# Layer 0's output turned by VectorE and DRAM, and layers 0 and 1 in another order of steps

## The chip, the cores and the metric

The kernel runs on one core of a Trainium2 chip. The metric is the device time of one execution, in microseconds (us). The profile is one execution taken by the hardware profiler. Engines are named as in the profile: PE is TensorE's matmuls, PEld its weight loads, DVE is VectorE, ACT is ScalarE, POOL is GpSimd, SP is SyncE, which here only issues DMAs.

## What is computed

Four layers of a graph network over 128 graphs of 64 nodes with 256 features each, all in float32. Every layer ends in a residual and a layer norm. The change concerns the first two:

```python
# layer 0: attention over a dense 64 x 64 adjacency
Wh = h @ W
e = leaky_relu(Wh @ a1 + (Wh @ a2)^T)          # masked where adj == 0
x = layernorm(x + softmax(e) @ Wh)
# layer 1: attention over a list of 512 edges (src, dst), 4 heads
Xq = H @ W_lin.T ; Xv = H @ W_val.T
e = (leaky_relu(Xq[src] + Xq[dst]) * a).sum(d) + log(adj[src, dst] + 1e-8)
attn = softmax of e over the edges of a src
x = layernorm(x + segment_sum(attn * Xv[dst], src) @ W_out.T)
# layer 2: two matmuls with batch norm over all rows; layer 3: two graph products and four LSTMs
```

Layer 2's batch norm needs all rows, so layers 0 and 1 are finished for all graphs before the rest of layer 2 runs.

## The kernel before

**Blocks.** The 8192 rows (128 graphs of 64 nodes) are cut into NQ = 16 blocks of QT = 512 rows, eight graphs in each. `A` is one large SBUF tile with a slot of 1024 floats per partition for each block. It holds each block's values as they pass through the layers; until a slot is needed, it also serves as scratch memory for the setup (`su`).

**Two layouts.** A matmul contracts over partitions. So the projections `h @ W` need their rows turned: features on partitions, rows along the free dimension. In *token-major* layout the rows are on partitions.

- `transposed` (L199 to L206) turns a block with TensorE: eight transposes of 128x128 (L204) into two PSUM banks, and two evictions by ScalarE (L205) into the tile `tT`.
- Layer 0's input for blocks 1 to 15 is turned otherwise. `load_x` (L126 to L135) loads the block twice: once token-major into `xin` (L128), and once into the block's slot of `A` in 32x32 squares (L135), by eight DMAs of 64 KB each, whose rows of 32 floats are put so that squares lie at their turned places. VectorE's transpose (L220 in `l0_a`) then turns each square in itself, which completes the turn.
- Layer 1's input, the output of layer 0, is turned by TensorE for all blocks (`l1_t`, L285).

**Steps of layer 0** for a block: `l0_a` turns the input; `l0_b` projects it (L230); `l0_c` makes the scores, starting with four TensorE transposes (L241), and their exponentials; `l0_d` turns those (L260); `l0_e` multiplies by them (L270), adds the residual (L273), takes the layer norm's statistics on VectorE, and lets GpSimd normalise into the slot of `A` (L83 and L97). `load_x(q + 2)` follows there.

**Steps of layer 1**: `l1_t` turns; `l1_qv` projects to queries (L295) and values (L298) in two halves; eight `l1_graph`, one per graph, gather the queries along the edges (L332) and apply a relu on ScalarE (L334); `reduce_heads` (called by `sums`, L323) sums it up. Over two blocks (BPS = 2) together, `l1_softmax`, `l1_sums` and `l1_weights` make the attention with scans on VectorE, turn it (L366), let GpSimd scatter it into a table in DRAM (four indirect DMAs, L378), and load the table back (`ld`, L384, two DMAs of 512 KB). `v_a` has GpSimd copy a block's attention from `ld` to `am` (L391), multiplies the values by it (L399) and empties the two banks on ScalarE (`yT`, L403). `v_b` multiplies by `W_out` (L413), adds the residual (L415), normalises on GpSimd and stores the block (L418). `v_c` is the first graph product of layer 2 (L433).

**Order.** For each block the loop at L659 goes through eight slots. Each slot runs one `l1_graph`, then the steps listed for it in `between`; a step belongs to the block named with it, so layer 0 runs two blocks ahead of layer 1's graphs, and `v_a` to `v_c` run three or four behind (LAG = 3). `step` chains TensorE: the instructions that a step puts on TensorE are issued after those of the step before (`tc.issue_after`). So TensorE follows the written order, while the framework's scheduler places the instructions on the other engines, each engine working in order.

**Buffers.** The PSUM banks named `m` are three (`bank`, `bufs=3`) and serve nearly every step. `z` has two banks for `l1_graph` and `v_c`. The tile `tT` has one buffer (`bufs=1`) in `work` for layer 0 and layer 1 together.

Of the kernel before, what the change touches and what calls it, by code (L numbers as in the profile page):

```python
# [8 lines left out]
F32 = mybir.dt.float32  # L9
# [8 lines left out]
P = 128  # L18
NB = 128
N = 64  # L20
D = 256
KD = D // P
HEADS = 4
# [3 lines left out]
NQ = 16  # L27
PQ = 4
QT = 512
# [12 lines left out]
def kernel(ctx: ExitStack, tc: tile.TileContext, i, out):  # L42
    nc = tc.nc
# [4 lines left out]
    dram = ctx.enter_context(tc.tile_pool(name="dram", bufs=1, space=DRAM))  # L48
# [3 lines left out]
    A = main.tile([P, NQ, 2 * QT], F32, name="A")  # L52
# [59 lines left out]
    with ExitStack() as two:  # L112
        wa = two.enter_context(tc.tile_pool(name="wa", bufs=1))
        values, ph = ExitStack(), ExitStack()
        vp = values.enter_context(tc.tile_pool(name="vp", bufs=1, side="right"))
        psm = values.enter_context(tc.tile_pool(name="psm", bufs=1, space=PSUM, side="right"))
        xp = ph.enter_context(tc.tile_pool(name="xp", bufs=2))
        work = ph.enter_context(tc.tile_pool(name="work", bufs=2))
        ps = ph.enter_context(tc.tile_pool(name="ps", bufs=1, space=PSUM))

        def bank(shape, name="m", bufs=3):
            return (psm if name == "m" else ps).tile([P] + shape, F32, name=name, bufs=bufs)

        xin = {}

        def load_x(q):  # L126
            xin[q] = xp.tile([P, PQ, D], F32, name="xin")
            nc.sync.dma_start(xin[q], x_view[q])  # L128
            if q:

                rows = i["x"][q * QT:(q + 1) * QT, :].rearrange("(j t) (k i f) -> i k t j f", t=32, k=KD, f=32)
                for n in range(4):
                    for k in range(KD):
                        to = A[n * 32:(n + 1) * 32, q, k * QT:(k + 1) * QT]
                        nc.sync.dma_start(to.rearrange("t (j f) -> t j f", f=32), rows[n, k])  # L135

        class su:

# [27 lines left out]
        for s in range(2):  # L166
            nc.sync.dma_start(bd[s * N:(s + 1) * N, s * N:(s + 1) * N], i["adj"])
        load_x(1)

        wq = wa.tile([P, KD, D + HEADS], F32, name="wq")  # L170
        wv = wa.tile([P, KD, D], F32, name="wv")
# [26 lines left out]
        def transposed(src, q=1):  # L198

            t = own(q, [P, KD, QT], "tT")  # L200
            for k in range(KD):
                p_ = bank([PQ, P])
                for c in range(PQ):
                    nc.tensor.transpose(p_[:, c, :], src[:, c, k * P:(k + 1) * P], ident)  # L204
                nc.scalar.activation(t[:, k, :], p_.rearrange("p c t -> p (c t)"), AF.Copy)  # L205
            return t  # L206

        def token_major(q):

            return A[:, q, :].rearrange("p (c d) -> p c d", c=PQ)  # L210


        L0 = {}

        def l0_a(q):
            L0[q] = {"x": xin.pop(q)}
            if q:

                L0[q]["xT"] = work.tile([P, KD, QT], F32, name="tT", bufs=1)
                nc.vector.transpose(L0[q]["xT"].rearrange("p k t -> p (k t)"), A[:, q, :])  # L220
            else:
                L0[q]["xT"] = transposed(L0[q]["x"], q)

        def l0_b(q):
            xT = L0[q]["xT"]
            wh = L0[q]["wh"] = own(q, [P, PQ, D + 2], "wh")
            for c in range(PQ):
                p_ = bank([D + 2])
                for k in range(KD):
                    nc.tensor.matmul(p_, xT[:, k, c * P:(c + 1) * P], w0[:, k, :],  # L230
                                     start=k == 0, stop=k == KD - 1)
                nc.scalar.activation(wh[:, c, :], p_, AF.Copy)

            sb = L0[q]["sb"] = own(q, [P, PQ, P], "sb")
            nc.scalar.activation(sb, wh[:, :, D + 1:].to_broadcast([P, PQ, P]), AF.Copy)

        def l0_c(q):
            wh, sb = L0[q]["wh"], L0[q]["sb"]
# [25 lines left out]
        def l0_e(q):  # L264
            x, wh, eT, ri = (L0[q][n] for n in ("x", "wh", "eT", "ri"))
            for c2 in range(2):
                p_ = bank([2, D])
                for c in range(2):
                    g = 2 * c2 + c
                    nc.tensor.matmul(p_[:, c, :], eT[:, g, :], wh[:, g, :D], start=True, stop=True)  # L270
                for c in range(2):
                    g = 2 * c2 + c
                    nc.vector.scalar_tensor_tensor(x[:, g, :], p_[:, c, :], ri[:, g:g + 1], x[:, g, :],  # L273
                                                   op0=OP.mult, op1=OP.add)
            layernorm(token_major(q), x, PQ, nc.gpsimd)
            L0.pop(q)
            if q + 2 < NQ:
                load_x(q + 2)


        L1 = {}

        def l1_t(q):
            L1[q] = {"xT": transposed(token_major(q)), "qs": [],
                     "v": vp.tile([P, PQ, D], F32, name="v", bufs=5)}  # L285

        def l1_qv(q, c2):
            xT, v = L1[q]["xT"], L1[q]["v"]

            sp = spads[q // BPS % 2].rearrange("p (s e x b d h) -> p s e x b d h", e=2, s=2, x=2, b=BPS, d=2)  # L290
            pv = bank([2, D])
            for c in (2 * c2, 2 * c2 + 1):
                pq = bank([D + HEADS])
                for k in range(KD):
                    nc.tensor.matmul(pq, xT[:, k, c * P:(c + 1) * P], wq[:, k, :],  # L295
                                     start=k == 0, stop=k == KD - 1)
                for k in range(KD):
                    nc.tensor.matmul(pv[:, c % 2, :], xT[:, k, c * P:(c + 1) * P], wv[:, k, :],  # L298
                                     start=k == 0, stop=k == KD - 1)

                qs = work.tile([P, 2, D], F32R, name="qs", bufs=6)
                L1[q]["qs"].append(qs)
                for s in range(2):
                    r, ro = slice(s * N, (s + 1) * N), slice((1 - s) * N, (2 - s) * N)
                    nc.scalar.activation(qs[r, s, :], pq[r, :D], AF.Copy)  # L305
                    nc.vector.tensor_sub(qs[ro, s, :], pq[r, :D], qs[r, s, :].bitcast(F32))  # L306
                    nc.scalar.activation(sp[r, s, c % 2, 0, q % BPS, c // 2, :], pq[r, D:], AF.Copy, scale=SLOPE)
            nc.scalar.activation(v[:, 2 * c2:2 * c2 + 2, :], pv, AF.Copy)
# [75 lines left out]
                nc.sync.dma_start(ld[S][s * N:(s + 1) * N], half)  # L384


        def v_a(q):
            S, b = divmod(q, BPS)
            v = L1[q]["v"]
            am = vp.tile([P, PQ * HEADS, N], F32, name="am")  # L390
            nc.gpsimd.tensor_copy(am.rearrange("p (e r) n -> p e r n", e=2),  # L391
                                  ld[S].rearrange("p n (e b r) -> p b e r n", e=2, b=BPS)[:, b])
            pY = [bank([KD, PQ, N]) for _ in range(2)]
            for c in range(PQ):
                for h in range(HEADS):
                    for s in range(2):
                        r = slice(s * N, (s + 1) * N)
                        r0 = (h % 2) * 64
                        nc.tensor.matmul(pY[s][r0:r0 + 64, h // 2, c, :], v[r, c, h * 64:(h + 1) * 64],  # L399
                                         am[r, (c % 2) * 2 * HEADS + c // 2 * HEADS + h, :], start=True, stop=True)  # L400
            yT = L1[q]["yT"] = vp.tile([P, KD, PQ, 2, N], F32, name="yT")
            for s in range(2):
                nc.scalar.activation(yT[:, :, :, s, :], pY[s], AF.Copy)  # L403
# [234 lines left out]
        LAG = BPS + 1  # L638
# [20 lines left out]
        for q in range(NQ):  # L659
            S = q // BPS - 1 if q % BPS == 0 else -1  # L660
            between = [
                [(l0_e, q + 1), (l0_a, q + 2)],
                [(sums, q if q else -1), (l1_softmax, S)],
                [(l1_sums, S), (l0_b, q + 2)],
                [(v_b, q - LAG - 1)],
                [(l1_weights, S), (l1_t, q + 1), (l0_c, q + 2)],
                [(sums, q), (l1_qv, q + 1, 0)],
                [(v_c, q - LAG - 1), (v_a, q - LAG)],
                [(l0_d, q + 2), (l1_qv, q + 1, 1)],
            ]  # L670
            for b in range(GQ):
                step(l1_graph, q, b)
                for do, n, *more in between[b]:
                    step(do, n, *more)
                if setup:
                    setup.pop(0)()
        sums(q)
        S = NQ // BPS - 1
# [56 lines left out]
        q = 0  # L735
        for do, n in [(v_b, NQ - LAG - 1), (v_c, NQ - LAG - 1)] + [
                (do, n) for n in range(NQ - LAG, NQ) for do in (v_a, v_b, v_c)]:
            do(n, *[False] * (do == v_c))
            up_block(q)
            q += 1  # L740
# [85 lines left out]
    work = ctx.enter_context(tc.tile_pool(name="work3", bufs=2, reuse_waits="tile"))  # L826
# [311 lines left out]
```

## Time and profile before

| | us |
|---|---|
| median of 3 runs | 2138.15 (2138.13 to 2138.42) |
| profiled execution: span | 2136.4 |
| layers 0 and 1, up to the last graph step | about 515 |
| one pair of blocks in the steady part (four in a row) | 61.25, 61.26, 61.25, 61.26 |
| TensorE busy in such a pair | 58.3 |
| VectorE, ScalarE, GpSimd busy in such a pair | 37.5, 40.9, 23.4 |

The granted clock is 1.00 in all four of these pairs. A pair is the unit to think in: the edge attention and its table come once for two blocks. The rest of the span, from about 515 us on, is layers 2 and 3, which the change doesn't touch, apart from one separate call of the attention's copy for the last three blocks.

### The profile page before, as it was taken

What the parts mean: (1) busy time and instruction counts of PE and PEld (TensorE: products, weight loads), DVE (VectorE), ACT (ScalarE), POOL (GpSimd) and SP (SyncE); (2) the same over time, 40 slices, a digit from 0 to 9 for tenths busy, and PEclk for the clock granted to TensorE, in tenths of its full rate; (3) what the DMA queues carried; (4) which work ended last, traced back from release to release, by engine and by line L of the source; (5) the groups of instructions that cost most, each with busy time, mean ns of one, the idle gap of its engine ahead of it and who ended that gap; (6) DMA issues with size and microseconds to landing.
All of it is one profiled execution on the core that took longest, in us unless ns stands there. A gap on an engine that the chain in (4) does not pass through costs nothing.

```text
span 2136.4 us, 29441 instructions
## 1 busy us (share of the span) xinstructions
PE 2060.7 (96%) x11343; PEld 1330.1 (62%) x11343; DVE 885.9 (41%) x2069; ACT 932.1 (44%) x1795; POOL 430.1 (20%) x569
## 2 busy tenths in 40 slices
PE   5999999998999989999999999999999999999998
PEld 4666767665544444585576576577467468468467
DVE  7456566654444343333234334324324324323213
ACT  2776666664339014334234334334334334333333
POOL 1134334332210010121112112113103103102012
PEclk8999999998999989999999999999999999999999
DMA  5244532322240021012112102103103102101001
GB/s 144 63 69 73 85 61 53 52 43 43 43 118 29 0 89 60 21 54 66 40 46 74 40 29 90 40 11 99 50 6 104 50 1 89 50 1 60 20 1 60
DMA packets 232636, 113.41 MB, mean 53 GB/s; under 512 B 150192, under 2 KB 215728, under 8 KB 232240
## 3 DMA queue, kind: packets, MB, share of 16 engines
q1 hardware_dynamic: 230640, 109.57, 20.2%
q8 instruction: 89, 1.46, 0.3%
q0 software_dynamic: 1024, 1.05, 0.2%
q10 hardware_dynamic: 832, 0.92, 0.1%
q14 instruction: 51, 0.42, 0.1%
HBM read 67.45 MB, written 44.04 MB: 52 GB/s over the span
## 4 chain that ended last, share of the span: by engine, by line
PE 86%; DVE 6%; ACT 4%; issue 2%; POOL 1%; DMA 1%; SPq 0%; POOLq 0%; DVEq 0%; ACTq 0%
PE l L994 36%; PE l L1000 20%; PE pz L784 5%; PE pz L719 5%; PE e L323 3%; PE g L933 2%; PE g L945 2%; PE m L295 2%; PE m L230 2%; PE z L332 2%; PE m L298 2%; PE g L878 1%; PE m L413 1%; PE m L270 1%; ACT u L334 1%
## 5 line engine op out<-in xcount | busy, mean ns | idle before, releaser
L994 PE MATMUL l<-H,wih 128*128 128x256 f32 (+2 forms) x2496 | 787.5, 470 | 1.8 <-ACT H L957 1.2
L994 PEld LDWEIGHTS l<-H,wih 128*128 128x128 f32 x2496 | 471.4, 190 | 286.2 <-issue 185.6
L1000 PE MATMUL l<-hid,whh 128*128 128x256 f32 (+2 forms) x1536 | 435.9, 437 | 0.0
L1000 PEld LDWEIGHTS l<-hid,whh 128*128 128x128 f32 x1536 | 291.8, 190 | 128.4 <-issue 61.2
L1006 ACT ACTIVATE gate_i<-l,bias 128x256 f32<-128x256 f32 (+2 forms) x176 | 100.3, 570 | 441.9 <-PE l L1000 374.2
L1010 POOL TENSOR_TENSOR cell<-gate_f,cell 128x256 f32<-128x256 f32 (+2 forms) x96 | 85.0, 885 | 726.0 <-ACT gate_f L1006 726.0
L1009 DVE TENSOR_TENSOR gate_i<-gate_i,gate_g 128x256 f32<-128x256 f32 (+2 forms) x96 | 49.6, 517 | 415.1 <-ACT gate_g L1006 415.0
L83 POOL TENSOR_TENSOR ln_rs<-ln_rs,mhalf 128x2 f32<-128x2 f32 (+2 forms) x97 | 82.0, 846 | 571.6 <-DVE ln_rs L95 570.7
L334 ACT ACTIVATE u<-z 128x1024 f32<-128x1024 f32 x128 | 130.3, 1025 | 63.3 <-PE z L332 62.3
L1006 ACT ACTIVATE gate_g<-l,bias 128x256 f32<-128x256 f32 (+2 forms) x176 | 100.3, 570 | 107.9 <-PE l L994 59.5
L1014 ACT ACTIVATE gate_g<-cell 128x256 f32<-128x256 f32 (+2 forms) x176 | 90.0, 511 | 86.9 <-DVE cell L1013 45.0
L1013 DVE TENSOR_TENSOR cell<-gate_i,gate_g 128x512 f32<-128x512 f32 (+2 forms) x80 | 48.2, 602 | 186.5 <-ACT gate_g L1006 186.4
L1006 ACT ACTIVATE gate_o<-l,bias 128x256 f32<-128x256 f32 (+2 forms) x176 | 99.3, 564 | 59.9 <-PE l L1000 54.0
L719 PE MATMUL pz<-A,w 128*128 128x512 f32 x256 | 113.1, 595 | 0.0
L332 PE MATMUL z<-gath_r,qs 128*128 128x512 f32 x256 | 100.4, 480 | 0.7 <-ACT u L334 0.4
L306 DVE TENSOR_TENSOR qs<-m,qs 64x256 fp32r<-64x256 f32 x128 | 54.0, 422 | 107.0 <-ACT qs L305 104.8
L719 PEld LDWEIGHTS pz<-A,w 128*128 128x128 f32 x256 | 47.9, 190 | 55.3 <-issue 53.3
L295 PE MATMUL m<-wq,tT 128*128 128x260 f32 x256 | 71.8, 403 | 7.8 <-ACT yT L403 5.4
L1006 ACT ACTIVATE gate_f<-l,bias 128x256 f32<-128x256 f32 (+2 forms) x96 | 51.1, 532 | 59.6 <-PE l L1000 59.1
L1023 DVE TENSOR_TENSOR hid<-gate_o,gate_g 128x256 f32<-128x256 f32 (+2 forms) x96 | 47.4, 493 | 61.2 <-ACT gate_o L1006 35.1
L721 DVE BATCH_NORM_STATS2 st<-pz 128x6 f32<-128x512 f32 x64 | 44.4, 697 | 59.5 <-PE pz L719 59.4
L1023 DVE TENSOR_TENSOR H<-gate_o,gate_g 128x512 f32<-128x512 f32 (+1 forms) x64 | 41.3, 645 | 66.6 <-PE l L994 46.1
(242 smaller groups left out, 2525.2 us busy)
## 6 DMA issues: line engine op xcount, KB each, us to landing
way<-st SPq DMA_DIRECT2D x59, 256.0 KB
st<-way SPq DMA_DIRECT2D x236, 64.0 KB
xin<-in_x SPq DMA_DIRECT2D x16, 512.0 KB
ld<-table SPq DMA_DIRECT2D x16, 512.0 KB
x_dram<-y SPq DMA_DIRECT2D x16, 512.0 KB
x2r<-x_dram SPq DMA_DIRECT2D x32, 256.0 KB
x_dram<-A SPq DMA_DIRECT2D x64, 128.0 KB
x3r<-x_dram SPq DMA_DIRECT2D x64, 128.0 KB
```

Source lines behind the costliest of these rows:

```text
L83: nc.gpsimd.tensor_tensor(dst, dst, mhalf[:, :n], OP.pow)
L295: nc.tensor.matmul(pq, xT[:, k, c * P:(c + 1) * P], wq[:, k, :], start=k == 0, stop=k == KD - 1)
L332: nc.tensor.matmul(z[:, k, :], L1[q]["qs"][c][:, s, k * P:(k + 1) * P], gath_r, start=True, stop=True)
L334: nc.scalar.activation(u, z, AF.Relu)
L719: nc.tensor.matmul(p_, w1[:, k, m * P:(m + 1) * P], A[:, q, k * QT:(k + 1) * QT], start=k == 0, stop=k == KD - 1)
L784: nc.tensor.matmul(p_, w2[:, k, m * P:(m + 1) * P], hidden(q, k), start=k == 0, stop=k == M1 - 1)
L994: nc.tensor.matmul(gates[n], wih[p][:, k, mw * P:(mw + 1) * P], Hw[:, k, :, s, :], start=k == 0, stop=not s and k == KD - 1)
L1000: nc.tensor.matmul(gates[n], whh[p][:, k, m * P:(m + 1) * P], hid[:, k], start=False, stop=k == KD - 1)
L1006: nc.scalar.activation(act[n], gates[n], AF.Tanh if n == "g" else AF.Sigmoid, bias=bias[:, p - 1, m:m + 1])
L1010: nc.gpsimd.tensor_tensor(cell[:, j], act["f"], cell[:, j], OP.mult)
L1014: nc.scalar.activation(act["g"], cell[:, j], AF.Tanh)
L1023: nc.vector.tensor_mul(Hw[:, jj, :, s, :] if over else new[:, jj], o, t)
```

## The change

Layer 1's input is turned in the manner of layer 0's, for blocks 2 to 15 (`TURN = 2`). When `l0_e` has normalised a block, it is written to DRAM (`x1_dram`, 512 KB), and read back as 32x32 squares by eight DMAs (`load_squares`) into the next block's slot of `A`, or, for the last two blocks, into a tile named `xin`. `l1_t` then turns the squares on VectorE. The eight transposes on TensorE and the two evictions on ScalarE are gone for these blocks. It is meant to take work from TensorE, and the new order to leave time for the round trip.

Layer 0's input of block 1 is now turned by TensorE like that of block 0. The squares of x for later blocks are loaded by `load_xT`, one block at a time, once the projection of the block before has been traced (in `l0_b`), since VectorE now puts the turned tile into the next block's slot instead of into `tT`.

In the order of steps `l0_e` and the next `l0_a` go from the first slot to the last slot of the block before; the second half of the queries from the last slot to the first of the next block; `l0_b`, `v_b`, `l0_c`, `l1_t`, `l1_weights`, `v_c` and `v_a` change places as the diff shows. GpSimd's copy of the attention becomes a step of its own, `v_am`, in the fourth slot; its product `v_a` is in the eighth.

```diff
@@ load_x
-            if q:
-                rows = i["x"][q * QT:(q + 1) * QT, :].rearrange("(j t) (k i f) -> i k t j f", t=32, k=KD, f=32)
-                for n in range(4):
-                    for k in range(KD):
-                        to = A[n * 32:(n + 1) * 32, q, k * QT:(k + 1) * QT]
-                        nc.sync.dma_start(to.rearrange("t (j f) -> t j f", f=32), rows[n, k])
+        TURN = 2
+        def load_squares(to, rows):
+            rows = rows.rearrange("(j t) (k i f) -> i k t j f", t=32, k=KD, f=32)
+            for n in range(4):
+                for k in range(KD):
+                    part = to[n * 32:(n + 1) * 32, k * QT:(k + 1) * QT]
+                    nc.sync.dma_start(part.rearrange("t (j f) -> t j f", f=32), rows[n, k])
+        def load_xT(q):
+            load_squares(A[:, q, :], i["x"][q * QT:(q + 1) * QT, :])
@@ setup: after load_x(1)
+        load_xT(2)
@@ l0_a
-            if q:
-                L0[q]["xT"] = work.tile([P, KD, QT], F32, name="tT", bufs=1)
-                nc.vector.transpose(L0[q]["xT"].rearrange("p k t -> p (k t)"), A[:, q, :])
-            else:
+            if q < TURN:
                 L0[q]["xT"] = transposed(L0[q]["x"], q)
+                return
+            t = A[:, q + 1, :] if q + 1 < NQ else work.tile([P, KD * QT], F32, name="tT", bufs=1)
+            nc.vector.transpose(t, A[:, q, :])
+            L0[q]["xT"] = t.rearrange("p (k t) -> p k t", k=KD)
@@ l0_b, at its end
+            if TURN <= q + 1 < NQ:
+                load_xT(q + 1)
@@ l0_e, after layernorm(token_major(q), x, PQ, nc.gpsimd)
+            if q >= TURN:
+                x1 = dram.tile([QT, D], F32, name="x1_dram", bufs=2)
+                nc.sync.dma_start(x1.rearrange("(c p) d -> p c d", p=P), token_major(q))
+                sq[q] = A[:, q + 1, :] if q + 2 < NQ else xp.tile([P, PQ, D], F32, name="xin").rearrange(
+                    "p c d -> p (c d)")
+                load_squares(sq[q], x1)
@@ l1_t
-            L1[q] = {"xT": transposed(token_major(q)), "qs": [],
-                     "v": vp.tile([P, PQ, D], F32, name="v", bufs=5)}
+            L1[q] = {"qs": [], "v": vp.tile([P, PQ, D], F32, name="v", bufs=5)}
+            if q < TURN:
+                xT = transposed(token_major(q))
...
+                return
+            xT = work.tile([P, KD, QT], F32, name="tT", bufs=1)
+            with tc.issue_after([t for t in nc.cur_bb.bb.instructions if t.engine == mybir.EngineType.DVE][-1]):
+                nc.vector.transpose(xT.rearrange("p k t -> p (k t)"), sq.pop(q))
...
@@ v_a is cut in two
-        def v_a(q):
+        def v_am(q):
             S, b = divmod(q, BPS)
-            v = L1[q]["v"]
-            am = vp.tile([P, PQ * HEADS, N], F32, name="am")
+            am = L1[q]["am"] = vp.tile([P, PQ * HEADS, N], F32, name="am")
             nc.gpsimd.tensor_copy(am.rearrange("p (e r) n -> p e r n", e=2),
                                   ld[S].rearrange("p n (e b r) -> p b e r n", e=2, b=BPS)[:, b])
+        def v_a(q):
+            v, am = L1[q]["v"], L1[q]["am"]
@@ the order of steps, one line for each of the eight slots
-                [(l0_e, q + 1), (l0_a, q + 2)],
-                [(sums, q if q else -1), (l1_softmax, S)],
-                [(l1_sums, S), (l0_b, q + 2)],
-                [(v_b, q - LAG - 1)],
-                [(l1_weights, S), (l1_t, q + 1), (l0_c, q + 2)],
+                [(l0_e, -1 if q else 1), (l0_a, -1 if q else 2), (l1_qv, q if q else -1, 1)],
+                [(sums, q if q else -1), (l1_softmax, S), (l0_b, q + 2)],
+                [(l1_sums, S), (v_b, q - LAG - 1)],
+                [(l0_c, q + 2), (l1_t, -1 if q else 1), (v_am, q - LAG)],
+                [(l1_t, q + 1 if q else -1), (l1_weights, S)],
                 [(sums, q), (l1_qv, q + 1, 0)],
-                [(v_c, q - LAG - 1), (v_a, q - LAG)],
-                [(l0_d, q + 2), (l1_qv, q + 1, 1)],
+                [(l0_d, q + 2), (v_c, q - LAG - 1)],
+                [(v_a, q - LAG), (l0_a, q + 3 if q + 4 < NQ else -1), (l0_e, q + 2),
+                 (l0_a, q + 3 if q + 4 == NQ else -1)],
```

More of the change, by code (lines that the diff above doesn't have):

```diff
@@ L128, in load_x @@
             nc.sync.dma_start(xin[q], x_view[q])
-            if q:
-                rows = i["x"][q * QT:(q + 1) * QT, :].rearrange("(j t) (k i f) -> i k t j f", t=32, k=KD, f=32)
-                for n in range(4):
-                    for k in range(KD):
-                        to = A[n * 32:(n + 1) * 32, q, k * QT:(k + 1) * QT]
-                        nc.sync.dma_start(to.rearrange("t (j f) -> t j f", f=32), rows[n, k])
+        TURN = 2
[7 more added lines that the diff above has]
+            load_squares(A[:, q, :], i["x"][q * QT:(q + 1) * QT, :])
+        sq = {}
         class su:
@@ L283, in l1_t @@
         def l1_t(q):
-            L1[q] = {"xT": transposed(token_major(q)), "qs": [],
-                     "v": vp.tile([P, PQ, D], F32, name="v", bufs=5)}
+            L1[q] = {"qs": [], "v": vp.tile([P, PQ, D], F32, name="v", bufs=5)}
+            if q < TURN:
+                xT = transposed(token_major(q))
+                L1[q]["xT"] = [[xT[:, k, c * P:(c + 1) * P] for c in range(PQ)] for k in range(KD)]
+                return
+            xT = work.tile([P, KD, QT], F32, name="tT", bufs=1)
+            with tc.issue_after([t for t in nc.cur_bb.bb.instructions if t.engine == mybir.EngineType.DVE][-1]):
+                nc.vector.transpose(xT.rearrange("p k t -> p (k t)"), sq.pop(q))
+            L1[q]["xT"] = [[xT[:, k, c * P:(c + 1) * P] for c in range(PQ)] for k in range(KD)]
         def l1_qv(q, c2):
@@ L294, in l1_qv @@
                 for k in range(KD):
-                    nc.tensor.matmul(pq, xT[:, k, c * P:(c + 1) * P], wq[:, k, :],
+                    nc.tensor.matmul(pq, xT[k][c], wq[:, k, :],
                                      start=k == 0, stop=k == KD - 1)
                 for k in range(KD):
-                    nc.tensor.matmul(pv[:, c % 2, :], xT[:, k, c * P:(c + 1) * P], wv[:, k, :],
+                    nc.tensor.matmul(pv[:, c % 2, :], xT[k][c], wv[:, k, :],
                                      start=k == 0, stop=k == KD - 1)
@@ L737 @@
                 (do, n) for n in range(NQ - LAG, NQ) for do in (v_a, v_b, v_c)]:
+            if do == v_a:
+                v_am(n)
             do(n, *[False] * (do == v_c))
```

## The prediction

> **What bounds the kernel now.** I read the page first for the engine that never rests, then the table by stage for one repeating stretch, then TensorE's timeline in it for the holes.
>
> ```profile
> PE 2060.7 (96%) x11343; PEld 1330.1 (62%) x11343; DVE 885.9 (41%) x2069; ACT 932.1 (44%) x1795; POOL 430.1 (20%) x569
> 333.25:394.50 61.25, 58.41 (x539) 42.94 (x539) 37.10 (x96) 40.90 (x91) 23.14 (x27) 1.00 0.29 55
> ```
>
> The second line is one pair of blocks, an even and an odd one, in the steady part of layers 0 and 1 (columns: stretch, length, busy time of PE, PEld, DVE, ACT, POOL, granted clock, DMA share, GB/s). TensorE works 58.4 of 61.25 us, ScalarE 40.9, VectorE 37.1. So TensorE sets the period; the time can only change by its work or by its holes. TensorE's timeline gives both:
>
> ```profile
> 358.81 0.60 PE L366 MATMUL m<-ident,e 128*128 128x128 f32 x4
> 359.25 0.60 PE L366 MATMUL m<-ident,dn 128*128 128x128 f32 x4
> 360.52 0.79 PE L204 MATMUL m<-ident,A 128*128 128x128 f32 x4 [0.67 <-issue]
> 362.00 0.65 PE L204 MATMUL m<-ident,A 128*128 128x128 f32 x4 [0.69 <-ACT tT L205]
> 362.99 0.66 PE L241 MATMUL m<-ident,sb 128*128 128x128 f32 x4 [0.33 <-DVE ln_mv L93]
> 373.92 1.15 PE L295 MATMUL m<-wq,tT 128*128 128x260 f32 x4 [0.56 <-ACT yT L403]
> 378.13 1.89 PE L270 MATMUL m<-wh,eT 128*128 128x256 f32 x8
> ...
> 390.70 1.03 PE L204 MATMUL m<-ident,A 128*128 128x128 f32 x8
> 391.58 0.60 PE L241 MATMUL m<-ident,sb 128*128 128x128 f32 x4
> ```
>
> In the odd block the eight transposes of L204 hold TensorE from 390.70 to 391.58, 0.88 us. In the even one they stand behind the attention's own transposes (L366), which hold two of the three PSUM banks named m, and three holes of 0.67, 0.69 and 0.33 us open round them. One more hole of 0.52 to 0.56 us per block stands ahead of the second half of the queries (L295), which waits until the two banks of the value product have been emptied (yT L403). Together 2.8 us of the pair.
>
> [...] L204 needs ScalarE's L205 (0.60 us) to leave PSUM, while L220 (1.25 us for 128x1024) has its input put in place by DMA. [...] No run here shows yet how a write fares behind the large table load, and my odd block rests on it.
>
> **The change, part by part.**
>
> *Removed.* For blocks 2 to 15 eight transposes each: 2 x 0.88 = 1.76 us of TensorE per pair, and four evictions of 0.60 on ScalarE, which isn't the bound (0). With them go the three holes by the attention's transposes, since l0_c's transposes move a step ahead and nothing else wants a bank there until the next block's queries some 2.6 us later (z 0.73, sums 1.85): 1.69 per pair.
>
> *Moved.* The queries' second half leaves the place behind the value product; now l0_e stands there and wants banks too, though its first half finds one free. I count half of the 1.08 us: 0.54. The copy of the attention on GpSimd (L391, 1.98 us) is a step of its own, four steps ahead of its product. GpSimd is busy 23 of 61 us and nothing on TensorE waited for this copy in this pair: 0. Sum of the gains: 1.76 + 1.69 + 0.54 = 4.0 us per pair, over seven pairs 28 us.
>
> *Start.* Block 1 of layer 0 is again turned by TensorE: eight transposes, in a stretch where TensorE has holes of 2 to 6 us, so 0. The 1.24 us VectorE transpose that stood on the chain of waits at 23.66 goes: 1.2 us gained.
>
> *Added.* A VectorE transpose of 1.25 us per block (37.1 + 2.5 of 57 us: not the bound), a write of 512 KB, and eight reads of 64 KB in 128-byte rows. They are the new wait: layer 0's output, GpSimd, DRAM, back, VectorE, queries. The lines for it, from the queue of SyncE, GpSimd, and the chain of waits:
>
> ```profile
> 376.78 3.33 SPq L384 DMA_DIRECT2D ld<-table  x2
> 384.48 2.17 POOL L97 TENSOR_SCALAR A<-xin,ln_rs 128x256 f32<-128x256 f32 x4
> 387.15 1.98 POOL L391 COPY am<-ld 128x1024 f32<-128x1024 f32 x1 [0.49 <-DMA ld<-table]
> 1181.36 0.34 SPq L863 DMA_DIRECT2D way<-st  x1
> 1183.37 1.73 SPq L865 DMA_DIRECT2D st<-way  x4
> 245.91 2.54 SPq L135 DMA_DIRECT2D A<-in_x  x4
> 246.46 3.19 DMA A<-in_x
> 0.72 4.86 DMA xin<-in_x
> ```
>
> From the start of l0_e's product (378.13) to its last normalised row (386.65) are 8.5 us. A 256 KB write is answered 2.0 us after its issue (1181.36 to 1183.37); a 512 KB load took 4.86; for the 512 KB write I estimate 2.6, with 4.9 as the far end. Eight reads at the 0.487 us median of one L135 issue take 3.9; the far end is the 0.68 of a crowded stretch (8.11 us for 12 issues). The last lands 1.2 us after its issue ends (249.65 against 248.45). With the transpose and 0.3 for handovers: 8.5 + 2.6 + 3.9 + 1.2 + 1.25 + 0.3 = 17.75 us.
>
> Against it stands TensorE's work between l0_e (now the last of step 7) and the queries of step 5 in the next block, from starts in the timeline: l0_e 1.54, six z of 0.73, half the queries 3.5, two sums of 1.85, l0_b 3.3, v_b 3.26, l0_c 0.35: 20.0 us in an odd block; an even one adds softmax 0.56 and the attention's transposes 0.88: 21.4. So there is slack of 2.3 and 3.7 us: an even block doesn't wait.
>
> The odd one has the table load in the way. It was issued 13.2 us after GpSimd's first scatter (363.54 to 376.78), 3.2 us of it two normalisation steps in between; without most of those some 11.6. In the new even block the first scatter comes about 3.7 us into step 4 (VectorE: transpose, reciprocal 1.73, first product 0.28), so the load is issued at 15.3 and, with 10.3 us from issue to landing (376.78 to 387.1)[...]. l0_e starts 11.7 us into that count (steps 4 to 7 by the same durations), so its rows are ready at 20.2: the write stands up to 4.2 us behind the table. Less the slack of 2.3, [...]TensorE waits some 1.5 us at the odd block's queries. Ends: [...]1.5 + 2.3 + 1.5 = 5.3 with the slow write and slow reads. Behind the waiting VectorE transpose stand the query differences (L306) and the next rows of layer 0; TensorE waits for those only after it waits for the transpose itself. Seven pairs: 10.5 us. Blocks 1 to 3 have no v_b yet (3.26 less cover): 3 us more.
>
> Sum: -28 - 1.2 + 10.5 + 3 = -15.7, so 2138 - 16 = **2122 us**.
>
> The loads of x for blocks 2 and later now wait for l0_b, about 12 us after l0_e, and are needed at 28 us: 16 us for 3.9 of issues and 1.2 of landing, behind the new reads. Hidden.
>
> **Rivals.**
> - *Nothing waits.* The write isn't held behind the table, and the banks at l0_e cost nothing: 4.0 + 0.5 per pair, 32 us with the start: 2106. For it: slack in both kinds of blocks. Against: L391 in the odd block started the moment the table landed, so that load is really in flight then. Chance 0.20.
> - *The wait eats the gain.* 4 us per pair, the middle of slow write and slow reads: 2136. Chance 0.06 for within 4 us of before.
> - *A longer wait takes the place of the holes.* [...]If the loads of x (3.9 us) go ahead of the reads, or a read stands behind the wait for the scatters, or GpSimd's rows come late because a scatter is ahead of them, the odd block waits 1.5 + 3.9 and the even one too by some 2: 6 to 8 per pair, so 2 to 4 net, 14 to 28 us slower; about 2155. For it: the cover is 20 us for a path of 18 with five engines in it. Against: slack of a few us in the even blocks. Chance 0.24.
>
> **The numbers.** The forecast (a wait of 0 to 3 us per pair) has 0.50. Faster: 0.50 + 0.20 = 0.70; same 0.06; slower 0.24. The range runs from just under the first rival, 2103, to 2150, which leaves out about half of the last one and a little below.
>
> **What would show it.** L204 on A drops from 128 matmuls to 16, on xin rises from 8 to 16; the holes at L366, L241 and behind yT shrink; TensorE busy per pair falls to about 56.6 and the pair to 58 to 59.5 us. A hole at L295 that ends on VectorE's transpose, in odd blocks alone, is the table load's; in every block it is the round trip itself. Wrong I would be if the path from l0_e to the turned tile takes over 22 us, or if the bank waits merely move to l0_e and l0_c.

## The result, and the profile after

| | before | after |
|---|---|---|
| median, us | 2138.28 | 2198.25 (2195.54 to 2202.32, four runs) |
| ratio | | 1.0281 [1.0263, 1.0299] |
| first head sums of layer 1 start at | 70.6 | 65.7 |
| last graph step of layer 1 starts at | 516.2 | 574.0 |

The change makes the kernel 60 us slower; the forecast was 16 us faster. The last two rows say where: the first sums come 4.9 us earlier than before, the last graph step 57.8 us later. So all of it is lost inside the loop of layers 0 and 1, and layers 2 and 3 add almost nothing.

The page's first part, and the row of the costliest groups that matters (line, engine, operation, tiles, count; then busy time and mean ns; then idle time ahead of it and what ended most of that). The line numbers are those of the changed kernel: L312 is the new VectorE transpose, L323 the queries (L295 before).

```profile
PE 2067.7 (94%) x11239; PEld 1332.1 (61%) x11239; DVE 898.1 (41%) x2082; ACT 920.4 (42%) x1769; POOL 413.0 (19%) x569
...
L323 PE MATMUL m<-wq,tT 128*128 128x260 f32 x256 | 81.6, 448 | 59.1 <-DVE tT L312 57.2
```

TensorE issues 104 matmuls fewer, yet is busy 7 us longer, and sits 57.2 us idle ahead of the queries, where it waits for the new transpose. The same in two pairs of blocks and in two short stretches of them (columns as in the prediction: stretch, length, busy PE, PEld, DVE, ACT, POOL, granted clock, which is the share of its full clock that TensorE was given, DMA share, GB/s):

```profile
196.07:265.96 69.89, 59.33 (x522) 42.97 (x522) 39.33 (x97) 39.24 (x87) 21.11 (x26) 0.94 0.46 93
265.96:336.69 70.73, 60.37 (x523) 43.55 (x523) 39.32 (x97) 39.34 (x87) 21.10 (x26) 0.93 0.47 92
...
260.50:265.96 5.46, 0.00 (x0) 0.00 (x0) 4.08 (x9) 1.65 (x8) 3.34 (x5) 0.69 0.35 116
265.96:271.04 5.08, 5.08 (x16) 4.20 (x17) 0.91 (x3) 1.47 (x5) 1.92 (x2) 0.66 0.02 6
```

A pair takes 70 us instead of 61.25. The third line is the hole: 5.46 us without a matmul. The fourth is the half of the queries and values that follows it: 5.08 us at a granted clock of 0.66. Before, the same four groups of matmuls took 3.42 us at 1.00 (333.18 to 336.60). So a hole can be paid for twice: by its length, and by slow matmuls behind it. In the four pairs from 196 to 478 us, every hole of 5.5 us is followed by slow matmuls (at 196.07, 265.96, 336.69 and 407.38, granted 0.50 to 0.66 over the next 5.08 us); of the four holes of 3.5 us two are (at 299.67 and 370.56, granted 0.66), and two aren't (230.26 and 441.75, granted 1.00). In a later run holes of only 1.9 us were followed by slow matmuls three times in five (shown with the half-size filler). What decides it isn't shown, and these runs give no shortest hole that counts.

How one pair adds up, for 265.96 to 336.69. TensorE's work should be 58.43 busy before, less 1.76 for the transposes, 56.67 us. It is busy 60.37, so 3.70 us are slow clock. Two holes at the transpose are 3.49 + 5.47 = 8.96 us. The rest, 1.4 us, is small waits. All four pairs on average: 70.35 us, with 3.35 us of slow clock.

Who holds the transpose? VectorE's timeline of the same pair, an even block and an odd one (start, length, operation, and in brackets VectorE's idle time before it with what ended it). Even and odd mean the loop's `q` here and below; the transpose in the steps of an even `q` belongs to block q + 1.

```profile
261.90 0.67 DVE L261 TENSOR_REDUCE mx<-e 128x4 f32<-128x512 f32 x1
...
264.29 0.18 DVE L267 RECIPROCAL ri<-sm 128x4 f32<-128x4 f32 x1 [1.14 <-ACT e L264]
264.66 1.25 DVE L312 STREAM_TRANSPOSE tT<-A 128x1024 f32<-128x1024 f32 x1 [0.19 <-issue]
...
295.59 0.69 DVE L261 TENSOR_REDUCE mx<-e 128x4 f32<-128x512 f32 x1
298.00 0.18 DVE L267 RECIPROCAL ri<-sm 128x4 f32<-128x4 f32 x1 [1.72 <-ACT e L264]
298.37 1.25 DVE L312 STREAM_TRANSPOSE tT<-A 128x1024 f32<-128x1024 f32 x1 [0.20 <-DMA A<-in_x]
```

SyncE's timeline has the reads of the squares for the same two blocks:

```profile
250.56 4.91 SPq L138 DMA_DIRECT2D A<-x_dram  x8
...
289.74 4.05 SPq L138 DMA_DIRECT2D A<-x_dram  x8
```

The transpose starts at once when `ri` is done, in both blocks. `ri` (L267) is the last VectorE operation of `l0_c`: the reciprocal of the softmax's sums, which ScalarE's exponentials (L264) must have made first. VectorE stands idle for it for 1.14 and 1.72 us with the transpose queued behind. In the even block the squares had been there long: their eight reads were issued by 255.47, and with 1.2 us to land (as measured before the change) the tile was complete at about 256.7 by this estimate, eight us before the transpose began. Of these eight us VectorE is idle for little more than one; in the rest it works off what stands ahead of the transpose: layer 1's layer-norm statistics, `l0_c`'s scores, and the attention's reciprocal and product. In the odd block the same working gives 295.0, more than three us before the transpose. In the odd block the name of a DMA in the bracket carries no weight: 0.20 us is the same handover as the 0.19 above it. All 14 blocks show a hole, in the waits of layers 0 and 1 (total us, times, longest):

```profile
PE m L323 <- DVE tT L312: 57.2, 14, 5.5
```

Two blocks differ. In the last one (transpose at 541.84) no `l0_c` is left to stand ahead, and the hole is only 0.67 us. In one early block (158.66) VectorE waits another 2.06 us after `ri` for the squares themselves; there the round trip is late.

### The profile page after: what moved, and what is told of

The parts are those of the page before. It is cut to its first block, busy times and chain, and to the rows that moved or that the text cites. A ratio compares the mean times of both kernels' runs of the same rounds, so it can differ in the third digit from the quotient of the medians.

```text
span 2193.8 us, 29463 instructions
## 1 busy us (share of the span) xinstructions
PE 2067.7 (94%) x11239; PEld 1332.1 (61%) x11239; DVE 898.1 (41%) x2082; ACT 920.4 (42%) x1769; POOL 413.0 (19%) x569
## 4 chain that ended last, share of the span: by engine, by line
PE 83%; DVE 7%; ACT 4%; DMA 3%; issue 3%; POOL 1%; SPq 1%; DVEq 0%; POOLq 0%; ACTq 0%
PE l L1027 35%; PE l L1033 19%; PE pz L817 5%; PE pz L750 5%; PE m L323 3%; PE g L966 2%; PE g L978 2%; PE m L326 2%; PE m L241 1%; PE g L911 1%; PE m L443 1%; PE z L360 1%; PE m L283 1%; PE e L351 1%; ACT u L362 1%
## 5 line engine op out<-in xcount | busy, mean ns | idle before, releaser
L323 PE MATMUL m<-wq,tT 128*128 128x260 f32 x256 | 81.6, 448 | 59.1 <-DVE tT L312 57.2
L323 PEld LDWEIGHTS m<-wq,tT 128*128 128x128 f32 x256 | 55.3, 223 | 84.5 <-DVE tT L312 70.8
L333 ACT ACTIVATE qs<-m 64x256 fp32r<-64x256 f32 x128 | 48.3, 377 | 68.7 <-PE m L323 67.4
L326 PE MATMUL m<-wv,tT 128*128 128x256 f32 x256 | 75.5, 423 | 0.0
```

Source lines behind the costliest of these rows:

```text
L323: nc.tensor.matmul(pq, xT[k][c], wq[:, k, :], start=k == 0, stop=k == KD - 1)
L326: nc.tensor.matmul(pv[:, c % 2, :], xT[k][c], wv[:, k, :], start=k == 0, stop=k == KD - 1)
```

## The experiments

Four theories stood against each other after that. **A**: the transpose's place on VectorE, behind `l0_c`'s softmax, makes the holes. **B**: the round trip through DRAM is too slow, and would make the holes from any place. **C**: much of the loss is the slow clock behind the holes. **D**: the written edge (`tc.issue_after` round the transpose) is to blame, and the scheduler would do better by itself. All ratios are against runs of the kernel before on the same chip (medians 2138.18, 2138.23 and 2136.36).

### No written edge

```diff
-            with tc.issue_after([t for t in nc.cur_bb.bb.instructions if t.engine == mybir.EngineType.DVE][-1]):
-                nc.vector.transpose(xT.rearrange("p k t -> p (k t)"), sq.pop(q))
+            nc.vector.transpose(xT.rearrange("p k t -> p (k t)"), sq.pop(q))
```

> The changed kernel without tc.issue_after round layer 1's VectorE transpose (L312), so that the scheduler alone places it. It then stands one place further ahead, before the reciprocal ri (L267), in four even blocks, and at the same place in the other ten. Theory A (the tile is long back from DRAM; the transpose only stands behind ri, which waits for ScalarE's exponentials): TensorE's wait at the queries falls by some 1.1 us in those four blocks and nowhere else, total about 2193. Theory B (the round trip through DRAM is late): nothing changes, 2198. Theory D (the written order edge alone is to blame, the scheduler would place it well): the waits go in all blocks, about 2120.

Measured: 2192.74 us, 1.0254 [1.0236, 1.0273]. The scheduler by itself puts the transpose behind `ri` too, but for four blocks, and TensorE still waits 50.2 us for it in 14 blocks:

```profile
PE m L322 <- DVE tT L311: 50.2, 14, 5.5
```

D falls, and the 2193 that A forecast came true.

### The new order alone

All blocks are turned by TensorE, as before the change; the order of steps, the early squares of x and GpSimd's copy as a step stay. Nothing is written to DRAM between the layers.

```diff
 l0_e
-            if q >= TURN:
+            if False:
 l1_t
-            if q < TURN:
+            if True:
```

> The new order of steps, with layer 1's input turned by TensorE in all blocks as before the change (no write to DRAM, no squares read back; layer 0's part of the change stays). Theories A and B both put the whole loss on the wait for the turned tile: with it gone the pair should take 61.25 less the 1.7 us of holes round the transposes and 0.5 of the bank hole, 59.0 us, total about 2122. Rival (the new order itself costs, by bank waits moved to l0_e and l0_c): 2138 or more.

Measured: 2125.85 us, 0.9939 [0.9920, 0.9957], faster than both kernels. One of its pairs:

```profile
239.35:299.80 60.45, 58.64 (x540) 42.96 (x539) 37.11 (x96) 40.89 (x91) 20.77 (x27) 1.00 0.39 73
```

TensorE does the same work as before (58.64 against 58.43 us), its holes come to 1.82 us instead of 2.84, and the clock is full. So the order of steps is worth 0.8 us per pair; 59.0 had been expected for it. Seven pairs make 5.6 us, and the start another 4.5 (the first sums at 66.1 against 70.6), 10.1 of the 12.3 us by which the last graph step starts earlier (503.9 against 516.2). The order is the good part of the change, and the turn through DRAM alone costs more than the 60 us.

### The hole filled with work

Eight source matmuls whose result nobody reads go ahead of the first half of the queries. They leave the wait for the transpose as it is, but keep TensorE busy in it.

```diff
+            if q >= TURN and c2 == 0:
+                warm = bank([E])
+                for _ in range(8):
+                    nc.tensor.matmul(warm, ident, gath, start=True, stop=True)
```

> The changed kernel with eight more matmuls of 128x512 (3.4 us of TensorE, into a bank that nobody reads) ahead of the first half of the queries of blocks 2 to 15, where TensorE waits for the turned tile: 48 us of work added. Theory C (part of the loss is TensorE's clock, granted at 0.66 for some 5 us after each hole): the work fits into the holes, the queries run at full clock, and 14 times 1.3 to 1.7 us are won: about 2177. Without C: 2198, or up to 2210 where the work doesn't fit.

Measured: 2205.85 us, 1.0317 [1.0298, 1.0336]; a miss. TensorE's timeline shows why, and that the point itself holds:

```profile
264.81 7.13 PE L322 MATMUL m<-gath,ident 128*128 128x512 f32 x16
271.78 1.04 PE L327 MATMUL m<-wq,tT 128*128 128x260 f32 x4
```

Each of these source matmuls in float32 stands as two in the trace, and the eight take 7.1 us, twice the 3.4 of the forecast, which was an estimate, and more than the hole of 5.5 or 3.5 that they were to fill. Even so, 14 x 7.0 = 98 us of added work cost only 7.6 us, and the queries behind ran at full speed. I had sized the filler wrongly, so it ran again at half the size:

```diff
-                for _ in range(8):
+                for _ in range(4):
```

> As e3_warm with four matmuls in the source instead of eight. Float32 matmuls run as two instructions here, so e3 put 7.1 us into each hole, not 3.4: 5 us a pair more than the holes of 5.5 and 3.5 hold. Four take 3.5 us and fit. Theory C (the slow clock after each hole costs 1.3 to 1.7 us): 2177, that is 20 us less than the changed kernel with 49 us of work more. Without C: 2198.

Measured: 2179.96 us, 1.0197 [1.0180, 1.0214]. With 14 x 3.5 = 49 us of useless matmuls added, the kernel is 18 us faster than the changed one. C holds for this much: of the 60 us, about 18 are slow clock, near the 7 x 3.35 = 23 of the trace. Not all slow matmuls are gone. The filler leaves holes of 1.93 or 1.94 us in five even blocks, and the queries behind three of them (at 191.29, 260.47 and 397.11) still run at 0.66, here with the stretch behind the second:

```profile
260.47 1.76 PE L327 MATMUL m<-wq,tT 128*128 128x260 f32 x4 [1.93 <-DVE tT L312]
...
260.47:265.55 5.08, 5.08 (x17) 4.14 (x17) 0.94 (x3) 1.47 (x5) 1.92 (x2) 0.66 0.02 6
```

The changed kernel has slow queries behind 11 of its 14 holes. So C can't be the whole: 42 us stay, with eight of eleven slow stretches gone.

### The transpose ahead of `ri`

The transpose goes right behind the row maximum (`mx`), and `ri` and the VectorE work of `l1_weights` behind it. Nothing else moves.

```diff
+        def behind_turn(do, *args):      # issues do's instructions after the last transpose
...
 l0_c, at its end
-            nc.vector.reciprocal(ri, sm)
+            L0[q]["sm"] = sm             # for q >= TURN, l0_r(q) does it behind the transpose
...
-                [(l1_t, q + 1 if q else -1), (l1_weights, S)],
+                [(l1_t, q + 1 if q else -1), (l0_r, q + 2), (weights_behind, S)],
```

> The changed kernel with the order on VectorE forced: layer 1's transpose right behind the maximum mx of l0_c (L261), and ri (split off from l0_c) and l1_weights' VectorE work behind the transpose. No transfer is touched. Theory A: TensorE's wait at the queries falls from 5.5 to about 1.7 us in even blocks and from 3.5 to about 1.3 in odd ones (there the tile lands about then), [...]the pair about 60.5 us instead of 69.7, total about 2135. Theory B (the round trip is late): the waits stay, now ending on the DMA, total about 2198 or more, since ri is then late too.

Measured: 2171.00 us, 1.0149 [1.0125, 1.0172]: nearly half of the loss is gone (27 of 60 us), not the nearly all that A expected. TensorE's and VectorE's timelines, even block first, then odd:

```profile
258.05 1.15 PE L338 MATMUL m<-wq,tT 128*128 128x260 f32 x4 [1.71 <-DVE tT L326]
...
292.95 2.10 PE L338 MATMUL m<-wq,tT 128*128 128x260 f32 x4 [4.64 <-DVE ri L230]
```

```profile
291.65 1.25 DVE L326 STREAM_TRANSPOSE tT<-A 128x1024 f32<-128x1024 f32 x1 [3.23 <-DMA A<-in_x]
```

The even hole shrinks from 5.48 to 1.71 us, as A said. The slow matmuls don't go with it in every block, though: behind it and a second hole of 1.24 us, for `rd`, they stay in three of five even blocks (at 194.09, 396.18 and 464.01, where four of the values' matmuls take 2.07 or 2.08 us instead of 1.13). The odd hole doesn't shrink: in four pairs it is 3.08, 4.64, 4.09 and 2.56 us, against 3.49 (TensorE's bracket names `ri`, which ends just behind the transpose; the transpose is what it needs). But now VectorE itself stands idle for 3.23 us, and what it waits for is really the DMA. With the softmax out of the way, a second limit is just behind it, and SyncE's timeline shows it:

```profile
273.54 3.36 SPq L427 DMA_DIRECT2D ld<-table  x2
277.01 5.46 SPq L307 DMA_DIRECT2D x_dram<-A  x1
...
285.49 4.04 SPq L138 DMA_DIRECT2D A<-x_dram  x8
```

The write stands behind the table load. Its mere issue takes 5.46 us, where the same write in an even block takes 0.38, and the reads can start only 8.5 us after it, against 3.0 there (243.38 to 246.41). This is the longest case: in the six odd blocks with a table load the issue takes 1.43 to 5.46 us, and the reads start 5.2 to 8.5 us after the write. In the changed kernel itself, where `ri` makes everything later, the odd write at 284.88 was issued in 0.39 us and its reads followed 4.9 us later. This is the step that the prediction feared in the odd block, where it was an estimate with no run behind it, now seen.

### The transpose ahead of all of `l0_c`'s VectorE work

On top of the last kernel, in even blocks (even q in the loop) the transpose goes ahead of `l0_c`'s VectorE work.

```diff
-                [(l0_c, q + 2), (l1_t, -1 if q else 1), (v_am, q - LAG)],
-                [(l1_t, q + 1 if q else -1), (l0_r, q + 2), (weights_behind, S)],
+                [(l1_t, q + 1 if q and q % 2 == 0 else -1), (c_behind, q + 2), (l1_t, -1 if q else 1), (v_am, q - LAG)],
+                [(l1_t, q + 1 if q % 2 else -1), (l0_r, q + 2), (weights_behind, S)],
```

> As e4_turn_after_max, but in even blocks layer 1's VectorE transpose stands ahead of all of l0_c's VectorE work; odd blocks as in e4. Theory A (in even blocks the tile is back 4 us before TensorE needs it, and only the place on VectorE decides): the two even holes of e4 (1.7 us for tT, 1.2 us for a PSUM bank held until at is done) go, 2.9 us a pair; odd blocks stay at 4.6 us plus slow matmuls. Total about 2150. Rival (the even tile is late as well): VectorE waits on the DMA ahead of l0_c, the hole stays, 2171 or more.

Measured: 2163.68 us, 1.0121 [1.0101, 1.0141]. This is 7 us better, not the 20 expected. The even block's wait for the transpose is gone, but waits for PSUM banks come in its place, mostly of 0.69 us and less: 11.0 us in all for `e`, `rd` and `at`, which VectorE reaches behind the transpose. In the last kernel TensorE waited 10.6 us for the transpose and 7.8 for `rd`. The odd one waits 2.4 to 4.0 us in the steady part, and once, early, 7.8. So the remaining loss is mostly the odd blocks'.

### The table load behind the reads

On top of that, the table load of a pair is issued behind the reads of the squares in the next odd block, so that the write no longer stands behind it, and the attention's copy of that block moves to the seventh slot.

```diff
+        def l1_load(S):
-                nc.sync.dma_start(ld[S][s * N:(s + 1) * N], half)
+                with tc.issue_after(reads[-1]):      # the last read of squares
+                    nc.sync.dma_start(ld[S][s * N:(s + 1) * N], half)
...
-                [(sums, q if q else -1), (l1_softmax, S), (l0_b, q + 2)],
+                [(sums, q if q else -1), (l1_softmax, S), (l1_load, q // BPS - 1 if q % 2 else -1), (l0_b, q + 2)],
```

> As e5_turn_first, with the two 512 KB table loads (ld) issued on SyncE behind the eight square reads of the odd block instead of ahead of the write to DRAM, and the attention's copy (v_am) of odd blocks moved from the fourth slot to the seventh. [...]the odd hole of 4.6 us and the slow matmuls after it shrink to about 1 us, the pair to about 59 us, total about 2108. Rival (the odd block is late for another reason, GpSimd's rows or the reads themselves): 2145 or more, with the gap between write and reads still over 6 us.

Measured: 2158.34 us, 1.0094 [1.0078, 1.0111]. Far from the 2108 that would have followed if the table were the last obstacle. SyncE's timeline and TensorE's:

```profile
274.40 0.38 SPq L308 DMA_DIRECT2D x_dram<-A  x1
...
279.06 4.04 SPq L138 DMA_DIRECT2D A<-x_dram  x8
283.20 3.68 SPq L431 DMA_DIRECT2D ld<-table  x2
286.98 8.34 SPq L138 DMA_DIRECT2D A<-in_x  x8
```

```profile
286.99 1.14 PE L340 MATMUL m<-wq,tT 128*128 128x260 f32 x4 [1.29 <-DVE tT L328]
...
295.73 1.16 PE L448 MATMUL m<-am,v 64*64 64x64 f32 x64 [1.71 <-POOL am L437]
```

The second limit is what it seemed: with the table out of the way, the write is issued in 0.38 us (1.74 in the same pair of the kernel before it), the reads follow 4.7 us later instead of 6.5, and the odd hole falls to 1.3 us from 2.5. But the wait only moves. The table now lands late, GpSimd waits 52 us in all for it (28.5 before), and TensorE 5.2 us for GpSimd's copy; and the squares of x need 8.34 us to issue behind the table. In even blocks TensorE now waits some 2 us for layer 0's turn (L242 here), 8.2 in all:

```profile
242.03 1.25 DVE L242 STREAM_TRANSPOSE A<-A 128x1024 f32<-128x1024 f32 x1
...
243.42 3.73 PE L251 MATMUL m<-w,A 128*128 128x258 f32 x16 [2.16 <-DVE A L242]
```

The late issue of the squares isn't the cause. VectorE never stands idle for them: in this kernel the turn is queued behind layer 0's statistics and the edge softmax, and in the kernel before it ran ahead of them (at 234.24). It is A's trap again, at another place. Why the scheduler moved it isn't shown.

### The round trip only where nothing stands in its way

Only odd-numbered blocks go through DRAM (their turn falls in even q, where no table load is in flight), with the transpose first on VectorE. The others are turned by TensorE.

```diff
 l0_e (to the kernel of the transpose ahead of all)
-            if q >= TURN:
+            if q >= TURN and q % 2:
 l1_t
-            if q < TURN:
+            if q < TURN or q % 2 == 0:
```

> As e5_turn_first, but only the odd-numbered blocks (3, 5, ... 15), whose transpose falls in even blocks, go through DRAM and VectorE; the even-numbered ones are turned by TensorE, so that no write stands behind the table load and there is half the added traffic. [...]the pair of e2_order_alone (60.4 us) less 0.9 of transposes and some 0.5 of bank holes, 59 us, total about 2116, faster than both kernels and than e2 (2126). Rival (the traffic itself costs more than the transposes are worth): 2126 or more.

Measured: 2130.13 us, 0.9971 [0.9961, 0.9982]. It isn't the 2116 expected, and 4 us above the order alone, whose last graph step (503.9) it also misses by 4 (508.1). A pair takes 61.06 us (195.13 to 256.19) against 60.45. TensorE's timeline has the reason:

```profile
239.69 1.15 PE L338 MATMUL m<-wq,tT 128*128 128x260 f32 x4 [0.69 <-DVE e L266]
241.35 1.56 PE L341 MATMUL m<-wv,tT 128*128 128x256 f32 x6 [0.52 <-DVE rd L415]
243.25 1.15 PE L338 MATMUL m<-wq,tT 128*128 128x260 f32 x4 [0.34 <-DVE at L417]
```

The transpose is in time. But its 1.25 us on VectorE push back what VectorE does next: the scores `e`, and the attention's `rd` and `at`, all of which read PSUM banks that the queries need. Holes of 0.69, 0.52 and 0.34 us, together 1.55, stand against the 0.88 us of transposes and the 0.94 of holes round the attention (0.17, 0.35 and 0.42) that the order alone has here. By this account the turn through DRAM would about break even; that the pair is 0.6 us longer, I can place only in part.

### The same transfers, the transpose behind `ri` again

As the last kernel in what goes through DRAM, but with `l0_c`, `ri` and the transpose in the places of the change.

```diff
 to the changed kernel
-            if q >= TURN:
+            if q >= TURN and q % 2:
...
-            if q < TURN:
+            if q < TURN or q % 2 == 0:
```

> As e8_half, but with the transpose at the changed kernel's own place on VectorE, behind the reciprocal ri. Transfers as in e8_half. Theory A: every even block waits 5.5 us for tT and then runs its queries at the slow clock (1.7), as in the changed kernel, though its tile has long landed: 7 x 7 = 50 us over e8_half, about 2166. Theory B (the round trip is late): the same as e8_half.

Measured: 2160.42 us, 1.0106 [1.0092, 1.0120]. The holes are back, five of the seven at full length (the first is 4.03 us, the last 0.96). One of them, from the timelines of SyncE, VectorE and TensorE, with the reads and the transpose ahead of it:

```profile
235.63 4.04 SPq L138 DMA_DIRECT2D A<-x_dram  x8
...
249.78 1.25 DVE L312 STREAM_TRANSPOSE tT<-A 128x1024 f32<-128x1024 f32 x1 [0.19 <-issue]
...
251.08 2.10 PE L323 MATMUL m<-wq,tT 128*128 128x260 f32 x4 [5.46 <-DVE tT L312]
```

The same blocks make the same round trip in both kernels, and 30 us lie between them: 4.3 us on average for each of the seven blocks, by the place of one transpose on VectorE among `l0_c`'s work. The 50 expected were too many: the holes come to 32.3 us and the six slow stretches behind them to about 10, an estimate, but the last kernel's 11.2 us of bank waits (`e`, `rd`, `at`) are gone again. In these blocks B is dead and A is shown. In the others both hold one behind the other: A's wait first, B's as soon as A's is taken away.

**What stays open.** The kernel with the softmax and the table out of the way still loses 20 us to the kernel before. I have not separated how much of that is crowding of the DMA engines (their share from 200 to 470 us is 0.35 before, 0.37 with the order alone and 0.52 in that kernel; the round trips add 14.7 MB in all) and how much the moved order. The early blocks, with single holes of 7.1 and 7.8 us in the first two kernels of the earlier transpose, were not studied.

## Why the prediction was wrong

- **What bounds the kernel**: right. TensorE still sets the period, and the time went by its work and its holes.
- **The transposes removed**: right. L204 (now L214) runs on A 16 times instead of 128, on xin 16 instead of 8, as foreseen.
- **The holes closed**: direction right, size a little too large. Without the new waits and the slow clock the pair of 265.96 would have 56.67 + 1.4 = 58.1 us, a gain of 3.2 instead of 4.0. GpSimd's copy at 0 was right: no TensorE wait for it in this pair.
- **The start**: too small, 4.9 us instead of 1.2.
- **The path of the round trip**: nearly right. From `l0_e` (238.32) to the landed tile (about 256.7) it took 18.4 us, where 8.5 + 2.6 + 3.9 + 1.2 = 16.2 were forecast. TensorE came for it at 260.5, so an even block had 3.8 us left for the 1.25 of the transpose. An even block needn't have waited.
- **The step that failed** is the last term of that sum, "0.3 for handovers", which assumes that VectorE starts the transpose when the tile lands. I listed what is queued *behind* the waiting transpose and didn't ask what stands *ahead* of it. The diff had the answer: `l1_t` now comes right after `l0_c`, with an edge that puts it behind the last VectorE instruction traced, and that is `ri`. Instead of 0.3 the term was 8.0 us in the even block (256.7 to 264.66) and 3.4 in the odd one (295.0 to 298.37).
- **The same move, counted on one side only.** That "l0_c's transposes move a step ahead" I took as a gain, for the holes round L366, and of those one of 0.16 us is left in this pair. The move also puts `l0_c`'s softmax, with its way over ScalarE and back, just in front of the new transpose.
- **The table load**: the wait of 1.5 us in odd blocks wasn't what TensorE felt in the changed kernel, because `ri` was later still. With the tile there at 295.0 and TensorE coming at 296.2, the transpose of 1.25 us would by itself have left almost no hole in that block. That the write would stand behind the table was right, and shown once the transpose was moved ahead of `ri`: 5.2 to 8.5 us from write to first read instead of 2.6.
- **The price of a hole** was mis-sized: I counted idle time alone. With the slow clock behind them the two holes of a pair, 8.96 us, cost 12.3.
- **The marker was wrong.** It said of a hole at the queries that "in every block it is the round trip itself". The hole is in every block and isn't the round trip. A wait that names the transpose says only that the transpose was last, not what held it. The other sign, a path of over 22 us from `l0_e` to the turned tile, did come: 27.6 us in the even block (238.32 to 265.91) and 24.2 in the odd one. There too the excess was the queue on VectorE.
- **The rivals.** The longer wait was on the right side with 14 to 28 us, but by another cause (the order on SyncE and GpSimd), and none of the rivals held VectorE's own queue. So the range ended at 2150.

The sum as it is: 57.2 us of holes and 7 x 3.35 = 23 of slow clock lost, 7 x 3.2 = 22 gained, 4.9 gained at the start, together 53 us; measured 57.8 at the last graph step. Some 4 us have no place in it.

## What to carry to other kernels

When an instruction moves to another engine, ask first what stands ahead of it in that engine's order and what *that* waits for; a path summed over transfers and durations holds only if the engine is free when the data lands. A wait taken away shows the next one behind it, so an odd and an even block with the same hole may need two different cures, and a change made of an order and a mechanism is best run in its halves: here the order alone was 12 us faster than before, while the mechanism that it was written for cost 72. And work taken from the busiest engine is worth only what the other engine's added time doesn't give back: here the transpose on VectorE, in time and with no table in its way, brought 1.55 us of bank waits for 1.8 us of matmuls and holes.

## What the runs showed of the hardware

- In the changed kernel a hole on TensorE of 5.5 us was followed each time by about 5 us at a granted clock of 0.50 to 0.66 (at 265.96, with 0.66, they took 1.7 us more than the same work at 1.00: 5.08 against 3.42); one of 3.5 us only at times, and in the kernel with the half-size filler one of 1.9 us was three times in five. 49 us of useless matmuls in the holes made the kernel 18 us faster.
- The issue of one 512 KB write on SyncE took 5.46 us right behind the issue of a 1 MB load in rows of 128 bytes (0.1 us after its end, at 277.01 in the first kernel of the earlier transpose), 1.74 us when it came 2.0 us after it (278.85 in the next one), and 0.38 or 0.39 us in the changed kernel, where it came 4.3 us after it or later.
- The filler's source matmuls in float32 stand as two each in the trace: eight of 128x512 are x16 and take 7.1 us. TensorE's transposes stand as one each: eight are x8 (1.03 us at 390.70 before the change).
